# Unread products between the steps that end two attention stages, and two VectorE steps in another order

## The chip, the core and the metric

The kernel runs on one core of a Trainium2 chip. The core has a matrix engine (TensorE, "PE" in the profile, with its weight loads as "PEld"), a vector engine (VectorE, DVE), a scalar engine (ScalarE, ACT), a general engine (GpSimd, POOL) and a queue engine (SyncE, SP) that here only issues DMAs. The engines run side by side, each through its own list of instructions in order, and wait for each other by semaphores. The metric is device microseconds (us) of one execution of the whole program, the median of three.

## What is computed

Two transformer layers over 8 sequences of 1024 tokens with 128 features, in float32:

```python
x = x + attn0(layernorm(x))    # 8 heads of 32, softmax over all 1024 keys, K and V through a rank-64 latent
x = x + ffn0(layernorm(x))     # 14 experts, the best two per token, gelu, weighted sum, clip
x = x + attn1(layernorm(x))    # 16 heads of 8, linear attention, causal: cumulative sums of k v^T
x = x + ffn1(layernorm(x))     # 8 experts, the best one per token with a capacity, relu
```

The router of each expert layer takes the logits of a token, picks one or two experts, and gives every token a place in the expert's rows.

## The kernel before

**Four stages in a row.** The first attention (lines 203 to 839) works through blocks of 512 queries; its steps are laid out half-step by half-step by a hand-written table. Beside it runs the end of each sequence: output projection, norm, router. The first expert layer (`tiles0`, line 903) then works through 72 tiles of 256 rows. The second attention (lines 1049 to 1588) works through 32 pairs of 128-token chunks, and the second expert layer (`tiles1`, line 1599) through 36 tiles of 256 rows.

**How tokens get to the experts.** A token's normalised row is written to DRAM at a row number that depends on its expert and on its rank among that expert's tokens: `rows_in` in the first layer, `rows1` in the second. These moves are indirect DMAs on GpSimd, one for each chunk of 128 tokens (and each of the two choices in the first layer), in `move` (lines 602 and 1426). Their row numbers are made by `places` (588 and 1408) on VectorE: `at` in the first layer, `where1` in the second. Each expert's rows are then cut into tiles of 256, and `expert_tables` (117) makes from the counts of all tokens a table of each tile's first row and expert (`row_j`, `exp_j`). SyncE reads `row_j` to fetch a tile (`fetch`, `fetch1`), VectorE reads `exp_j` to copy the expert's weights beside it (`stage`, `stage1`). The first fetch and the first staging of each expert layer wait for the last of the moves.

**The two ends.** The end of the first attention (806 to 839) finishes the last 512 tokens. A loop over four chunks divides by the softmax's sums on VectorE (818, 819), projects on TensorE (`f.project`, 451), and gathers the norm's statistics (`norm.stats`, 271). Then come the norm's power (on GpSimd), the scaled rows (`scaled`), their transposes (`turned`, 304), and the router's pieces in the order of `choice` (617): logits, the first and second choice, counts, ranks, places, softmax weights. The eight moves left over by `places` are issued last (838). The first step of `tiles0` makes the tables.

The end of the second attention (1549 to 1588) runs the last pairs, then routes the last sequence in two halves of four chunks, `first` and `second`, each a `Route` (1336) with the pieces `logits`, `choose`, `count`, `rank`, `places`, `softmax`, `keep_top`. `scatter(4)` issues four moves. `tiles1` begins with its tables.

**What sets the order.** In the attentions and in the tile loops the order of TensorE and VectorE is the program's order (`manual_schedule`). At the first tables (line 911) it is left to the scheduler, at the second (1607) it is the program's.

Names in the profile: `op` is the projection's result, `tp` and `px` are transposes, `lg` logits, `rk` ranks, `tot` the counts summed over partitions, `both_t` the transposed table, `ph` and `py` the first and second product of an expert, `xr` a fetched tile, `wt` its expert's weights.

## Time and profile before

| | us |
|---|---|
| median of three executions | 2041.25 (2039.91 to 2042.38) |
| the profiled execution | 2055.6 |
| its span, first to last instruction | 2053.8 |
| TensorE busy, share of the span | 1941.6, 95% |
| VectorE, ScalarE, GpSimd busy | 1376.3, 1107.8, 1201.0 |
| granted TensorE clock, mean over the span | 0.955 of full speed |
| `ph` of an expert of the second layer (L1645), 288 products | 69.9, 386 ns each |

How to read it: the profile divides the span into 40 equal slices of 51.3 us. For each engine a digit gives the busy share of a slice in tenths (9 is 90% or more), and the row PEclk gives the clock that TensorE was granted, in tenths of full speed. TensorE's products are pipelined, so their durations overlap and a "busy" TensorE is not one at its peak. A row of the timeline gives the start, the duration (from the first to the last of the merged instructions), the engine, the line, the operation, what it writes and reads, partitions by elements, how many instructions were merged, and in brackets how long the engine was idle before and what released it.

### The profile page before, as it was taken

What the parts mean: (1) busy time and instruction counts of PE and PEld (TensorE: products, weight loads), DVE (VectorE), ACT (ScalarE), POOL (GpSimd) and SP (SyncE); (2) the same over time, 40 slices, a digit from 0 to 9 for tenths busy, and PEclk for the clock granted to TensorE, in tenths of its full rate; (3) what the DMA queues carried; (4) which work ended last, traced back from release to release, by engine and by line L of the source; (5) the groups of instructions that cost most, each with busy time, mean ns of one, the idle gap of its engine ahead of it and who ended that gap; (6) DMA issues with size and microseconds to landing.
All of it is one profiled execution on the core that took longest, in us unless ns stands there. A gap on an engine that the chain in (4) does not pass through costs nothing. (4 is left out here: it accounts for less than half of the span.)

```text
span 2053.8 us, 45114 instructions
## 1 busy us (share of the span) xinstructions
PE 1941.6 (95%) x17340; PEld 1002.5 (49%) x17340; DVE 1376.3 (67%) x3551; ACT 1107.8 (54%) x2338; POOL 1201.0 (58%) x1312
## 2 busy tenths in 40 slices
PE   7999999999999999999999998699499999996997
PEld 3333333333333333333333333599367666665897
DVE  6677768768767767767766776476457666654453
ACT  3555555555565555555565554366357666551443
POOL 1465656767766767767667775422455556624455
PEclk9999999999999999999999998799789999986999
DMA  7000000000000000000000000344222211101331
GB/s 240 1 2 2 1 2 4 8 8 10 8 8 9 8 8 9 8 8 9 8 8 12 8 9 27 97 132 136 62 75 81 78 43 48 51 23 52 106 107 58
DMA packets 49406, 80.92 MB, mean 39 GB/s; under 512 B 13225, under 2 KB 32112, under 8 KB 49056
## 3 DMA queue, kind: packets, MB, share of 16 engines
q0 software_dynamic: 17552, 41.03, 6.0%
q1 hardware_dynamic: 28240, 28.97, 4.9%
q10 hardware_dynamic: 3392, 7.95, 1.3%
q8 instruction: 140, 2.29, 0.5%
q14 instruction: 82, 0.67, 0.1%
HBM read 42.08 MB, written 35.96 MB: 38 GB/s over the span
## 5 line engine op out<-in xcount | busy, mean ns | idle before, releaser
L352 DVE TENSOR_REDUCE nmp<-big 128x1 f32<-128x512 f32 x1000 | 641.7, 682 | 280.6 <-PE st L388 236.7
L391 ACT ACTIVATE e<-st 128x512 f32<-128x512 f32 x1000 | 544.2, 595 | 479.9 <-PE st L388 425.0
L216 POOL TENSOR_TENSOR e<-e 128x512 f32<-128x512 f32 x488 | 604.0, 1268 | 52.8 <-PE num L405 52.7
L348 PE MATMUL big<-kT,qT 32*128 32x512 f32 x2000 | 625.9, 641 | 0.7 <-DVE nmp L352 0.4
L388 PE MATMUL st<-qT,kT 32*128 32x512 f32 x2000 | 533.5, 590 | 0.0
L405 PE MATMUL num<-e,v 128*32 128x512 f32 x3064 | 301.6, 465 | 3.1 <-ACT nums L434 1.8
L216 POOL TENSOR_TENSOR outT<-nums,dens 128x64 f32<-128x64 f32 x248 | 80.5, 325 | 343.3 <-DVE dens L423 258.1
L388 PEld LDWEIGHTS st<-qT,kT 32*128 32x128 f32 x2000 | 214.8, 192 | 5.1 <-issue 3.0
L387 PE MATMUL st<-nb,ones_h 3*128 3x512 bf16 x1000 | 212.7, 385 | 0.4 <-ACT e L391 0.4
L405 PEld LDWEIGHTS num<-e,v 128*32 128x32 f32 x3064 | 61.6, 108 | 292.4 <-issue 272.3
L348 PEld LDWEIGHTS big<-kT,qT 32*128 32x128 f32 x2000 | 192.0, 183 | 21.3 <-DVE nmp L352 17.3
L387 PEld LDWEIGHTS <-ones_h 3*128 3x128 bf16 x1024 | 50.9, 91 | 308.4 <-issue 302.6
L1122 POOL DMA_INDIRECT got<-rows_out,found x128 | 126.3, 987 | 93.7 <-PE tp L1157 36.5
L603 POOL DMA_INDIRECT rows_in<-xn,at x128 | 129.8, 1014 | 33.6 <-issue 24.9
L423 DVE RECIPROCAL dens<-dens 128x64 f32<-128x64 f32 x248 | 130.1, 536 | 16.5 <-ACT dens L418 16.4
L405 PE MATMUL den<-e,ones 128*32 128x512 f32 x1032 | 140.7, 608 | 0.0
L1667 POOL DMA_INDIRECT out_x<-y,to x72 | 78.9, 1096 | 68.2 <-DVE y L1665 51.2
L1648 ACT ACTIVATE g<-ph,wt 128x256 f32<-128x256 f32 x144 | 63.6, 474 | 86.9 <-PE ph L1645 83.2
L1083 POOL TENSOR_TENSOR rs<-ve,mhalf 128x2 f32<-128x2 f32 x64 | 46.3, 724 | 90.8 <-DVE ve L1081 65.9
L970 POOL DMA_DIRECT2D rows_out<-y x68 | 39.5, 581 | 94.5 <-DVE y L967 87.3
L1177 ACT ACTIVATE qm<-qk,cst 128x256 f32<-128x256 f32 x128 | 54.6, 496 | 53.9 <-DVE qk L1174 33.2
L1427 POOL DMA_INDIRECT rows<-row,where x64 | 63.8, 997 | 30.7 <-issue 14.3
(289 smaller groups left out, 2976.4 us busy)
## 6 DMA issues: line engine op xcount, KB each, us to landing
xr<-rows SPq DMA_DIRECT2D x36, 257.0 KB
xr<-rows_in SPq DMA_DIRECT2D x72, 128.0 KB
rows_out<-y POOLq DMA_DIRECT2D x68, 128.0 KB
nb<-part SPq DMA_DIRECT2D x384, 1.0 KB
blob<-in_blob ACTq DMA_DIRECT2D x8, 578.0 KB
blob<-in_blob SPq DMA_DIRECT2D x1, 4494.0 KB
x<-in_x SPq DMA_DIRECT2D x8, 512.0 KB
rows<-nil ACTq DMA_DIRECT2D x9, 257.0 KB
```

Source lines behind the costliest of these rows:

```text
L216: return tc.keep_in_program_order(f(*args, **kw))
L348: nc.tensor.matmul(ps, lhsT=qTs[n][r, qc * P:(qc + 1) * P], rhs=kTs[n][r, kb * BLK:(kb + 1) * BLK], start=True, stop=True,)
L352: nc.vector.tensor_reduce(nmps[n][:, h, qc, kb:kb + 1], ps, AX.X, ALU.max, negate=True)
L387: nc.tensor.matmul(st, lhsT=ones_h[r3, :], rhs=nbs[n][r3, cols], start=True, stop=False)
L388: nc.tensor.matmul(st, lhsT=kTs[n][r, kc * P:(kc + 1) * P], rhs=qTs[n][r, cols], start=False, stop=True)
L391: nc.scalar.activation(e[:, h, :], st, AF.Exp, scale=SCALE0)
L405: nc.tensor.matmul(vds[key][32 * h:32 * h + 32, cols], lhsT=ones[:, :HD0] if den else vs[b][:, kc, c0:c0 + HD0], rhs=e[:, h, cols], start= ...
L423: nc.vector.reciprocal(s[:, cols], s[:, cols])
L603: ins = nc.gpsimd.indirect_dma_start(out=rows_in, out_offset=bass.IndirectOffsetOnAxis(ap=ats[k][:, j:j + 1], axis=0), in_=xn[:, c0 + j, : ...
L1122: ins = tc.keep_in_program_order(nc.gpsimd.indirect_dma_start(out=gots[p][:, i, k, :], out_offset=None, in_=rows_out, in_offset=bass.Indir ...
L1427: ins = nc.gpsimd.indirect_dma_start(out=rows1, out_offset=bass.IndirectOffsetOnAxis(ap=at[:, c:c + 1], axis=0), in_=row[:, c, :], in_offs ...
L1667: ins = nc.gpsimd.indirect_dma_start(out=out_rows, out_offset=bass.IndirectOffsetOnAxis(ap=at[:, i:i + 1], axis=0), in_=y[:, i, :], in_off ...
```

## The change

A helper `keep_busy(bank, n)` issues `n` products on TensorE into one PSUM bank: bf16, 128 rows by 128 columns of weights, 512 moving columns, both operands read from the tile of ones. Nothing reads the bank. The helper is called

- in the loop that ends the first attention, with 2, 5, 5 and 14 products after the four projections, and with 13 after the logits (39 in all);
- in `expert_tables`, with 14 products after the sum of the counts and with 52 (first layer) or 42 (second) after the table's transposes;
- at the end of the second attention, with 5 products after the first half's logits and 11 after the second half's.

That makes 105 products at the first end and 72 at the second. The first tables are put under the program's order for TensorE and VectorE. At the second end, `second.logits()` is called after `first.places()` and `scatter(4)` instead of before them.

```diff
+    ones_b = ones.bitcast(BF16)
+
+    def keep_busy(bank, n):
+
+        for _ in range(n):
+            nc.tensor.matmul(
+                bank.rearrange("p (a b) -> p a b", a=2), lhsT=ones_b[:, :P],
+                rhs=ones_b.unsqueeze(1).to_broadcast([P, 2, 2 * P]), start=True, stop=True,
+            )
+
...
-    def expert_tables(tab, psum, ptag, counts, ne, nt):
+    def expert_tables(tab, psum, ptag, counts, ne, nt, unread, fill):
...
         nc.tensor.matmul(tot, lhsT=ones, rhs=counts, start=True, stop=True)
+        keep_busy(unread, 14)
...
         for i in range(2):
             nc.tensor.transpose(ps[:, i, :], both[:, i:i + 1], ident)
+        keep_busy(unread, fill)
...
         num, den = (vds.pop((n, qb, d)) for d in (False, True))
+        unread = sc.tile([P, BLK], F32, name="st", tag="st")
         for i in range(CPK + 1):
...
             if i:
                 f.project(i - 1, 1)
+                keep_busy(unread, (2, 2, 5, 5, 14)[i])
                 norm.stats(i - 1, 1)
...
         for piece in f.choice():
             piece()
+            if piece == f.logits:
+                keep_busy(unread, 13)
...
         if first == 0:
-            held0.tables = expert_tables(tab0, px, "px", counts, E0, NT0)
+            with tc.manual_schedule(engines={mybir.EngineType.PE, mybir.EngineType.DVE}):
+                unread = ph_ps.tile([P, BLK], F32, name="unread", tag="ph")
+                held0.tables = expert_tables(tab0, px, "px", counts, E0, NT0, unread, 52)
...
         first.logits()
+        unread = pa.tile([P, BLK], F32, name="a")
+        keep_busy(unread, 5)
         first.choose()
         first.exponentials()
...
         first.rank()
-        second.logits()
         first.places()
         scatter(4)
+        second.logits()
+        keep_busy(unread, 11)
         first.softmax()
...
                 with tc.manual_schedule(engines={mybir.EngineType.PE, mybir.EngineType.DVE}):
-                    tables.__dict__.update(expert_tables(tab, px, "px", counts1, E1, NT1).__dict__)
+                    unread = ph_ps.tile([P, BLK], F32, name="unread", tag="ph")
+                    tables.__dict__.update(expert_tables(tab, px, "px", counts1, E1, NT1, unread, 42).__dict__)
```

## The prediction

> **What bounds the kernel now.** I read three views: the page's 40 slices, one-microsecond windows of the clock, and the timeline of two stretches. The slices say where to look:

> ```profile
> PE   7999999999999999999999998699499999996997
> PEclk9999999999999999999999998799789999986999
> ```

> TensorE is busy everywhere except at the end of the first attention (25th and 26th slice), at the start of the second (29th: gathers, which the change leaves alone) and at the end of the second (37th). In the same places the granted clock falls. By one-microsecond windows it is 0.50 from 1276.97 to 1311.0, and, at the second end, from 1881.1 to 1908.4. Outside such stretches the page's tile loops run with TensorE full, so what is gained ahead of a loop moves the whole rest of the program.

> The timeline of the first end (start, duration, engine, line):

> ```profile
> 1279.02 0.80 PE L457 MATMUL op<-wo_sb,outT 128*128 128x128 f32 x2 [0.69 <-DVE outT L819]
> 1283.95 1.89 PE L480 MATMUL lg<-gate_sb,xT 128*128 128x14 f32 x8
> 1291.69 0.16 DVE L599 TENSOR_SCALAR at<-to 128x4 uint32<-128x4 f32 x1
> ...
> 1292.62 0.96 POOL L603 DMA_INDIRECT rows_in<-xn,at  x1 [4.30 <-issue]
> ...
> 1301.46 0.96 POOL L603 DMA_INDIRECT rows_in<-xn,at  x1 [0.30 <-issue]
> 1303.70 2.21 DVE L930 COPY wt<-blob 128x642 f32 x4 [8.57 <-DMA rows_in<-xn,at]
> 1305.98 1.43 PE L939 MATMUL px<-cst,xr 128*128 128x128 f32 x4 [11.26 <-DMA xr<-rows_in]
> 1307.20 2.06 PE L948 MATMUL ph<-xt,wt 128*128 128x256 f32 x4
> ```

> The reader should see a serial path: projection, norm, transposes, logits, choice, ranks, places (`at`), then eight moves on GpSimd, 1.26 us apart, their landing, the first fetch, the first tile. GpSimd ends last, not the table: `row_j` is written by 1295.0, nine microseconds before it is used. So only what makes `at` come earlier, or the tiles after 1305.98 shorter, counts.

> The second end:

> ```profile
> 1884.09 0.19 DVE L1406 TENSOR_TENSOR cand<-rk,oh 128x32 f32<-128x32 f32 x1 [1.24 <-PE rk L1404]
> 1885.76 0.19 DVE L1354 TENSOR_REDUCE mx<-lg 128x4 f32<-128x32 f32 x1 [1.48 <-PE lg L1350]
> 1886.57 0.17 DVE L1414 TENSOR_SCALAR where<-to 128x4 uint32<-128x4 f32 x1
> 1887.52 1.03 POOL L1427 DMA_INDIRECT rows<-row,where  x1 [5.90 <-ACT ex L1362]
> ...
> 1896.45 1.41 POOL L1427 DMA_INDIRECT rows<-row,where  x1 [0.30 <-issue]
> 1902.89 0.66 PE L1636 MATMUL px<-cst,xr 128*128 128x128 f32 x2 [8.89 <-DMA xr<-rows]
> 1904.84 3.62 PE L1645 MATMUL ph<-xt,wt 128*128 128x256 f32 x8
> 1908.55 1.89 PE L1645 MATMUL ph<-xt,wt 128*128 128x256 f32 x8
> ```

> Again eight moves in a row end last. Their first waits for `where`, and `where` waits only because `mx` of the second half's logits stands ahead of it on VectorE and itself waits 1.48 us for TensorE. The last two rows show one tile's products at half clock (3.62) and nearly full (1.89).

> **The change, part by part.** Everything is summed against the profiled execution (2055.6 us, span 2053.8).

> *Price of an unread product.* No row has a 128x128 bf16 product of 512 columns. The nearest:

> ```profile
> 1530.48 0.60 PE L1227 MATMUL a<-later,low 64*128 64x512 bf16 x2
> ```

> One of these lasts 387 ns (median), two 0.60 us, so they start 0.213 us apart at full clock; a pair at half clock (1491.46) takes 1.03 with 0.63 each, 0.40 apart. The weights (94 ns) load under the product before. Lower bound 0.213, upper 0.40; from that pair to the next line's product there are 0.265 a piece, which I keep as a middle. I take 0.213, if the clock is held.

> *Do they fit?* TensorE issues in order, so what follows a batch waits for it. First end: after each projection 2, 5 and 5 (0.4 to 1.1 us) stand before a projection that waits for `outT`, 1.90 us after the one before: hidden, 0.5 us left. Then 14 (3.0 us) from 1279.5 to 1282.5, where the transposes are due at 1282.5 (1282.80 less the 0.3 gained below): just hidden. 13 (2.8 us) after the logits, before `rk`, whose inputs take 3.0 us on VectorE: hidden, 0.3 left. 14 before `both_t` (due 3.7 us after `tot`): hidden. 52 (11.1 us) after `both_t` from about 1292.8: to 1303.9, first transposes due 1304.25. Second end: 5 (1.1 us) to 1881.3, transposes due 1881.4; 11 (2.3 us) to 1887.0, `rk` due 1886.7 but its second half due 1887.0: nothing; 14 hidden; 42 (8.9 us) from 1891.9 to 1900.9, transposes of tile 0 due 1900.6, but the tile products queue behind tile 1's transposes, which need a fetch at 1902.1: nothing. Every batch is within 0.5 us of its cover; without cover each 0.1 us per product costs 10.5 us at the first end's 105, 7.2 at the second's 72.

> *What the clock gives, first end.* Last projection pair 0.80 to 0.49 (the row at 1273.29 has that): 0.31. Transposes of a pair 0.66 to 0.38, logits 1.89 to 1.06 (eight passes at 1879.10, full clock): 1.11. From the end of the count's scan (1289.32) through `rk` to `cand` at 1290.13 there are 0.8, about 0.3 less at full clock. `at`, and with it all eight moves, come 1.7 us earlier. GpSimd is free for them: its five earlier moves end at 1288.3. Then the first tiles: two transpose pairs 0.3 each, `ph` of tile 0 2.06 to 1.03 (the row at 1312.24), `ph` of tile 1 1.82 to 1.03 in part: 2.1. Sum **3.8**.

> *The table's new place, first end.* The name says places go ahead of tables. In the compiled order of VectorE they do not: `grid` (0.61) and `tiles` (0.62) still stand between `ranks` and `at`, as before; only `lead`'s memset and a few table steps move behind `shares`. Had they moved, `at` would be some 0.9 us earlier. I count nothing; the table comes at most 0.3 later, with nine microseconds of cover (GpSimd's moves).

> *Second end, the order.* `second.logits` moves behind `first.places` and the four scatters. Its eight TensorE passes have the same place among TensorE's instructions, as neither step issues any there; the four scatters are the same GpSimd DMAs in the same order, and nothing passes SP's queue. On VectorE `mx` and `pr` move behind three operations of 0.2. `where` then ends 0.8 after `cand` instead of 2.65: 1.85. The clock gives `cand` another 0.45 (two transpose pairs 0.86 to about 0.44, `rk`). Sum 2.3 at the first move. `mx` loses nothing: its products end after `where`; were they done earlier it would lose 0.6. The moves stay back to back: `where` of the second half is at 1888.4, its move is not due before 1890.3.

> *Second end, tiles.* Tile 1's rows arrive 2.3 earlier, `ph` of tile 0 takes 1.73 instead of 3.62: 1.7 to 1.9. Sum **4.1**.

> Together 7.9: 2055.6 to 2047.7. The median shown is 14.4 lower (0.7%); scaled, 7.8, so 2041.25 becomes **2033.5**.

> [...]

> ```profile
> 1850.49:1853.91 3.42, 3.42 (x28) 2.88 (x26) 2.53 (x11) 0.47 (x2) 1.17 (x2) 0.98 0.00 0
> 1853.91:1857.32 3.41, 3.41 (x48) 1.61 (x50) 0.28 (x2) 0.88 (x3) 2.52 (x3) 0.50 0.22 77
> ```

> TensorE is busy for the whole first window, much of it logits of 8 columns, and the clock is halved in the next. So columns streamed count, not gaps. The unread products stream 512 each, and at the first end every 3.4 us hold at least 1.6 us of them. At the second, from 1881.3 to 1884.6 only transposes, `rk` and logits run; a window that falls on it loses the clock. Drops and rises here lie near multiples of 3.41 us from 1276.97, so I give this about 4 in 10; then the 11 take up to 1.7 more, and the 42 behind them end that much later, past their cover: 1.6 lost, 2035.1. [...] I keep 7.9 and put the rest into the range.

> **Rivals.** *Overrun (0.13).* If the pitch is 0.265, the 52 and 42 end 2.3 and 0.9 us after their covers and the others cost 1.0: gain 3.7, **2037.6**. For: covers are thin. Against: the pair's own pitch.

> *Cold filling (0.11, the slower side).* Place: the batches themselves. If the clock is already half when a batch starts, it runs at 0.40, and TensorE's order makes the chain wait. Each cold window puts a batch 1.7 us late; two windows at each end cost 6.8 and undo 3.3 of the clock's gain of 6: **2042**, and if they stay cold throughout, 0.19 on each of 177 less the covers is some 28 against 1.9 kept: 2067. It decides from a mean pitch of 0.29, that is a mean clock of 0.73 in the batches. For: in the rows 1853.9 to 1870.9 are cold right before the second end. Against: the clock is 1.00 when the first batch starts (1274), and dense products brought it back within 5 us at 1306 to 1311. With two cold windows it is about even, so I price this case at **2047**, three windows at each end.

> *Only the order counts (0.10).* Unread products neither hold nor delay: 1.9, **2039.4**. For: transposes and eight-column logits didn't hold it. Against: 512-column tiles do, throughout the first attention.

> **How the numbers follow.** Forecast as argued, 0.66, own range 2030 to 2037: the second attention has single cold windows (at 1604, 1652, 1700, 1748) whose number shifts with where it starts; one more or less is up to 1.7 us, and two either way is 3.4. Overrun and order-only reach 2039.4; one more cold window there 2041. Range 2029.5 to 2041, leaving out 0.11 for cold filling and a little below. About 0.2% (4 us) is what can be told from no change. Faster by more: 0.66 plus half of the overrun, 0.73; within: the rest of it and order-only, 0.16; slower 0.11.

> **What would show it.** Right: granted clock 1.00 from 1274 to the first tile; logits of eight passes near 1.06; first of the last eight moves near 1290.9; first tile `ph` 1.03; at the second end `where` before `mx`, first move 2.3 us sooner after its `rk`, `ph` of tile 0 near 1.75. Wrong: unread products 0.40 apart; first tile's transposes released by TensorE itself instead of by the fetch; a longer second attention with more cold windows than before.

## The result, and the profile after

The changed kernel takes **2034.91 us** (median of eight, 2027.27 to 2043.59), against 2040.58 (2037.13 to 2046.25) for eight executions of the kernel before that ran beside it. The two medians lie 5.7 us apart (0.9972); the estimated ratio on record is 0.9952, with a 95% interval of 0.9930 to 0.9973, which would be 9.8 us (5.5 to 14.3). So the change is faster, by 5 us or more, and this pair doesn't give the size any closer. The prediction said 2033.5, 7.8 less than before. The profiled execution of the changed kernel took 2033.86 us (span 2032.1, mean granted clock 0.976); that of before had a span of 2053.8 at 0.955.

The slices of the changed kernel, for TensorE and its clock:

```profile
PE   7999999999999999999999999999599999998997
PEclk9999999999999999999999999999789999988999
```

At the end of the first attention (25th and 26th slice) TensorE is now busy and the clock full. At the end of the second (37th) it is nearly so. The 29th slice, the gathers at the start of the second attention, is as before.

The timeline of the first end (start, duration, engine, line):

```profile
1276.76 3.18 PE L116 MATMUL st<-ones 128*128 128x512 bf16 x14
1280.85 1.06 PE L492 MATMUL lg<-gate_sb,xT 128*128 128x14 f32 x8
1286.41 0.62 DVE L136 TENSOR_TENSOR grid<-tot,cst 128x448 f32<-128x448 f32 x1
1287.07 0.62 DVE L141 TENSOR_REDUCE tiles<-grid 128x14 f32<-128x448 f32 x1
1287.61 0.16 DVE L611 TENSOR_SCALAR at<-to 128x4 uint32<-128x4 f32 x1
1288.53 0.96 POOL L615 DMA_INDIRECT rows_in<-xn,at  x1 [3.07 <-issue]
...
1290.92 11.38 PE L116 MATMUL unread<-ones 128*128 128x512 bf16 x52
...
1297.38 0.96 POOL L615 DMA_INDIRECT rows_in<-xn,at  x1 [0.30 <-issue]
1302.14 0.38 PE L957 MATMUL px<-cst,xr 128*128 128x128 f32 x2
1302.90 0.41 PE L957 MATMUL px<-cst,xr 128*128 128x128 f32 x2 [0.38 <-DMA xr<-rows_in]
1303.15 1.03 PE L966 MATMUL ph<-xt,wt 128*128 128x256 f32 x4
```

Four things to see. The logits take 1.06 instead of 1.89, the first tile's `ph` 1.03 instead of 2.06: full clock on the whole path (granted 1.00 from 1270 to 1310). Fourteen unread products of 0.379 us each take 3.18, so they start (3.18 - 0.379) / 13 = 0.2155 us apart. `grid` and `tiles` still stand ahead of `at`, as the prediction read from the compiled order. And the 52 end at 1302.3, where the second pair of tile 0's transposes still waits for its DMA until 1302.90: the long batch is covered, by little.

The timeline of the second end:

```profile
1865.04 0.19 DVE L1424 TENSOR_TENSOR cand<-rk,oh 128x32 f32<-128x32 f32 x1 [0.77 <-PE rk L1422]
1865.68 0.17 DVE L1432 TENSOR_SCALAR where<-to 128x4 uint32<-128x4 f32 x1
1865.73 4.22 PE L116 MATMUL a<-ones 128*128 128x512 bf16 x11
1865.91 0.19 DVE L1372 TENSOR_REDUCE mx<-lg 128x4 f32<-128x32 f32 x1
1866.63 1.03 POOL L1445 DMA_INDIRECT rows<-row,where  x1 [3.60 <-issue]
...
1875.74 0.96 POOL L1445 DMA_INDIRECT rows<-row,where  x1 [0.30 <-issue]
1883.76 0.60 PE L1658 MATMUL px<-cst,xr 128*128 128x128 f32 x4
1884.66 1.99 PE L1667 MATMUL ph<-xt,wt 128*128 128x256 f32 x8 [0.30 <-DVE xt L1660]
1886.71 1.89 PE L1667 MATMUL ph<-xt,wt 128*128 128x256 f32 x8
```

`where` now stands before `mx`, 0.64 us after `cand`. But the 11 unread products took 4.22 us where 2.5 was due. Windows of the clock show why. A window here is a step of 3.41 us, as the changes of the clock lie whole such steps apart: in the trace of before the stretches of one clock from 1276.97 on last 34.13, 143.36, 27.31, 6.83 and 20.48 us, which is 10, 42, 8, 2 and 6 steps, at 0.50, 1.00, 0.50, 1.00 and 0.50 in turn. The rows, like the pair of windows in the prediction, give start:end, length, TensorE busy, weight loads, three other engines, the granted clock, and last what the DMAs moved:

```profile
1862.68:1866.09 3.41, 2.78 (x18) 2.04 (x19) 2.30 (x14) 2.12 (x7) 0.35 (x1) 1.00 0.00 0
1866.09:1869.50 3.41, 3.41 (x10) 1.22 (x8) 1.98 (x13) 0.23 (x1) 2.26 (x3) 0.50 0.11 39
```

In the first of the two only transposes, `rk` and logits run, and at its very end the first two of the eleven; the next 3.41 us have half the clock, and the other nine fall into them. This is the loss to which the prediction gave 4 in 10.

### The profile page after: what moved, and what is told of

It reads as the page before. It is cut to its first block, busy times and chain, and to the rows that moved or that the text cites. A ratio compares the mean times of both kernels' runs of the same rounds, so it can differ in the third digit from the quotient of the medians.

```text
span 2032.1 us, 45469 instructions
## 1 busy us (share of the span) xinstructions
PE 1959.4 (96%) x17517; PEld 1007.4 (50%) x17517; DVE 1377.1 (68%) x3551; ACT 1107.7 (55%) x2338; POOL 1201.5 (59%) x1312
## 5 line engine op out<-in xcount | busy, mean ns | idle before, releaser
L399 PEld LDWEIGHTS <-ones_h 3*128 3x128 bf16 x1024 | 51.1, 91 | 308.9 <-issue 302.2
L1140 POOL DMA_INDIRECT got<-rows_out,found x128 | 126.4, 987 | 89.5 <-PE tp L1175 42.1
```

Source lines behind the costliest of these rows:

```text
L399: nc.tensor.matmul(st, lhsT=ones_h[r3, :], rhs=nbs[n][r3, cols], start=True, stop=False)
L1140: ins = tc.keep_in_program_order(nc.gpsimd.indirect_dma_start(out=gots[p][:, i, k, :], out_offset=None, in_=rows_out, in_offset=bass.Indir ...
```

## Where the 21.7 us between the two profiled executions lie

Each stage is measured between the same two instructions in both traces.

| stage (us) | before | after | difference |
|---|---|---|---|
| start to the first end's first reciprocal | 1272.6 | 1270.0 | -2.6 |
| first end: reciprocal to the first `py` | 38.5 | 35.1 | **-3.4** |
| first tiles, to the second attention's first gather | 144.9 | 144.5 | -0.4 |
| second attention, to the last sequence's first logits | 423.1 | 410.9 | -12.2 |
| second end: those logits to the second tile's `ph` | 29.4 | 26.2 | **-3.3** |
| second tiles, to the end | 145.2 | 145.4 | +0.2 |

The ends give 6.7 us. The 12.2 of the second attention lie where the change issues nothing. The experiments therefore had two questions: is the gain at the ends what the prediction says it is, and does the change do anything to the second attention?

## The experiments

They ran on three chips, a group on each, against the kernel before on the same chip (medians 2008.1, 2005.53 and 2055.55 us). The ratio is the measure, since two executions of one kernel differ by 10 us and more (before took 2001.44 to 2011.94 on the first chip). The lengths of the ends come from each run's profiled execution, and they repeat far better: the first end of a kernel that leaves it as it was took 38.5 to 38.6 us in four profiles, the second end 29.2 to 29.6 in three.

| run | ratio (95%) | us against before | clock got back, us | first end | second end |
|---|---|---|---|---|---|
| e0_before, nothing changed | | |  | 38.6 | 29.2 |
| a0_after, the change | 0.9961 (0.9947 to 0.9976) | -8.0 | 31.1 | 35.2 | 25.4 |
| e8_first, only the first end | 0.9979 (0.9966 to 0.9993) | -4.3 | 17.7 | 35.2 | 29.6 |
| e9_second, only the second end | 0.9983 (0.9965 to 1.0002) | -3.5 | 13.4 | 38.6 | 27.9 |
| e1_order, only the order | 0.9983 (0.9974 to 0.9991) | -3.4 | 0.2 | 38.6 | 27.9 |
| e2_fill, only the products | 0.9961 (0.9947 to 0.9975) | -7.8 | 28.3 | 35.1 | 26.5 |
| e3_narrow, products of 8 columns | 0.9970 (0.9957 to 0.9983) | -6.0 | 4.3 | 38.6 | 27.8 |
| e4_notable, none in the tables | 0.9980 (0.9967 to 0.9994) | -4.0 | 14.1 | 36.8 | 27.2 |
| e5_bridge, three more at the second end | 0.9939 (0.9922 to 0.9957) | -12.2 | 30.4 | 35.1 | 25.2 |
| e6_places, both `at` ahead of the table | 0.9961 (0.9950 to 0.9972) | -7.8 | 28.2 | 35.9 | 25.3 |
| e7_both, the last two together | 0.9966 (0.9955 to 0.9976) | -6.8 | 26.2 | 34.3 | 24.9 |
| e10_best, the same with a longer batch | 0.9959 (0.9943 to 0.9975) | -8.4 | 33.1 | 34.3 | 27.2 |

(The third column is the ratio less one, times the median of before in that group; the medians taken directly differ from it by up to 2 us. The fourth is from all executions: each one's span times one less its granted clock is the clock that it lost, and the column says how much less the median is than that of before, which is 88.3 us in the group of a0_after, e8_first, e9_second and e10_best, 72.3 in that of e1_order, e2_fill, e3_narrow and e5_bridge, and 70.1 in the other. It is good to about 2 us, as the clock is on record to three digits.)

The fourth column separates the kernels far better than the times do. In the profiles of before the clock is half for 34.1 us at the first end and 27.3 us at the second, which is 17.1 and 13.7 us of lost clock, 30.7 in all. The kernels with the wide products at both ends got back 26 to 33 us, e8_first 17.7, e9_second 13.4, and the order alone 0.2. Only part of it is time, as TensorE waited through much of the half clock (11.26 us ahead of the first tile's transposes at the first end, 8.89 at the second, in the prediction's lines).

### The change and its two halves: a0_after, e8_first, e9_second

a0_after is the change itself. e8_first leaves the second end as it was:

```diff
-        keep_busy(unread, 14)
+        if ne == E0:
+            keep_busy(unread, 14)
...
-        keep_busy(unread, 5)
...
+        second.logits()
         first.places()
         scatter(4)
-        second.logits()
-        keep_busy(unread, 11)
...
-                    tables.__dict__.update(expert_tables(tab, px, "px", counts1, E1, NT1, unread, 42).__dict__)
+                    tables.__dict__.update(expert_tables(tab, px, "px", counts1, E1, NT1, None, 0).__dict__)
```

e9_second does the reverse: no products in the first end's loop, after its logits or in its tables, whose order is again the scheduler's.

> The changed kernel itself on this chip, beside its parts. If the ends are all of it: first end near 35.1 against 38.6 before, second end 25.1 when no window of the clock is lost there and 26.2 when the one ahead of the ranks is, so 7.0 to 8.0 us below the median of before. If the unread products also change the second attention's windows for the better, 10 us or more below; if for the worse, less than 5.

> Only the first end's unread products and its hand-written order; the second end as before. Ends alone: first end 35.1, second end 29.2, so 3.5 us below before. If a first end that is earlier shifts the second attention's windows: anything from 0 to 8 below. Cold filling: none of it saved.

> Only the second end's part: the order and its unread products; the first end as before. Ends alone: first end 38.6, second end 25.1 to 26.2, so 3.3 to 4.3 below before, and together with the first end's run the sum of the two is the whole change within 1.5 us. If the two parts help or hinder each other, the sum is off by 3 or more.

Measured: 8.0 us for the whole, 4.3 and 3.5 for the halves, 7.8 in sum. The halves add up, though e9_second's interval reaches from -7.2 to +0.4 us, so that the times alone test this weakly; the clock got back adds up as well (17.7 and 13.4 against 31.1). The whole has the size of its two ends in its own profile (38.6 - 35.2 and 29.4 - 25.4: 7.4). In a0_after no window is lost at the second end, and that end is 4.0 us shorter: what the prediction summed for a held clock was 4.1.

e9_second shows the other case in its clearest form. Its windows (columns as above):

```profile
1867.90:1871.31 3.41, 2.03 (x24) 1.52 (x23) 1.77 (x8) 0.65 (x2) 0.90 (x2) 1.00 0.13 43
1871.31:1874.72 3.41, 3.41 (x13) 2.11 (x13) 2.95 (x18) 1.88 (x5) 0.92 (x2) 0.50 0.00 0
1874.72:1878.13 3.41, 3.41 (x18) 3.13 (x17) 0.92 (x6) 0.75 (x2) 0.39 (x1) 0.50 0.00 0
1878.13:1881.54 3.41, 3.41 (x10) 1.21 (x9) 1.95 (x12) 0.23 (x1) 2.57 (x3) 0.50 0.22 77
1881.54:1884.95 3.41, 3.41 (x21) 1.95 (x20) 2.19 (x11) 0.00 (x0) 1.84 (x2) 1.00 0.25 81
```

The clock is halved for exactly three windows of 3.41 us. TensorE counts as busy in all three. The first two hold the batch of five and the start of the eleven among transposes, ranks and logits and do not bring the clock back; the third, filled by most of the eleven, does. What the slow eleven delay can be read from the timeline of the same run: the second half's ranks, its places, and with them the fifth move:

```profile
1877.63 4.45 PE L116 MATMUL a<-ones 128*128 128x512 bf16 x11
1881.61 0.96 POOL L1440 DMA_INDIRECT rows<-row,where  x1 [0.30 <-issue]
1883.13 0.17 DVE L1427 TENSOR_SCALAR where<-to 128x4 uint32<-128x4 f32 x1
1884.07 0.96 POOL L1440 DMA_INDIRECT rows<-row,where  x1 [1.49 <-issue]
1886.82 9.23 PE L116 MATMUL unread<-ones 128*128 128x512 bf16 x42
1895.89 0.60 PE L1653 MATMUL px<-cst,xr 128*128 128x128 f32 x4
```

GpSimd waits 1.49 us for `where` (0.30 between moves is its usual step), and tile 0's transposes start right behind the 42. That end took 27.9 us, 2.5 more than a0_after's and as much as with the order alone (e1_order, 27.9): in this execution the products of the second end bought nothing. It is the prediction's rival of cold filling, at one end and in one execution: still faster than before, by what the order gives, and not slower.

### The order and the products apart: e1_order, e2_fill

e1_order is the kernel before with this alone:

```diff
-        second.logits()
         first.places()
         scatter(4)
+        second.logits()
```

e2_fill is the change without it: `second.logits()` and the eleven stand again ahead of the places.

> The kernel before, with only the second half's logits moved behind the first half's places and scatters on VectorE; no unread products. Stage lengths of the profile are compared: the first end from the first reciprocal of the divide loop to the first py of the expert tiles (38.5 us before, 35.1 changed), the second end from the last sequence's first logits to the second tile's ph (29.5 before, 26.2 changed). Clock theory: first end stays 38.5, second end 27.6 (1.9 less), clock 0.50 at both ends; whole program about 2 us less, not to be told from no change. Rival, only the order counts: the whole difference between the two kernels, 6 to 10 us, is already here.

> The changed kernel with the second half's logits back ahead of the first half's places; the unread products stay. Clock theory: first end 35.1, second end 27.1 if the clock is held and 28.1 if it is lost for a window, 5 to 6 us less than before as a whole. Rival, only the order counts: both ends as before, no gain.

From the last sequence's first logits to the start of `where` there are 7.47 us before, 5.64 with the order alone, 6.21 with the products alone and 5.17 with both. So the order is worth 1.83 at half clock, as the prediction had it (1.85), but only 1.04 once the clock is full (6.21 to 5.17); the products are worth 1.26 without the order and 0.47 with it. The sum is safe, the shares depend on which is taken first. The order cannot carry the gain: in e1_order's profile the end is 1.3 us shorter and the clock is lost as before, and over all executions the order alone gets back 0.2 us of clock where the products alone get back 28.3. The ratio of the run with the products alone is as good as that of the whole change.

### Does any product hold the clock? e3_narrow

Each unread product is replaced by two with 8 moving columns:

```diff
-        for _ in range(n):
-            nc.tensor.matmul(
-                bank.rearrange("p (a b) -> p a b", a=2), lhsT=ones_b[:, :P],
-                rhs=ones_b.unsqueeze(1).to_broadcast([P, 2, 2 * P]), start=True, stop=True,
-            )
+        for _ in range(2 * n):
+            nc.tensor.matmul(bank[:, :8], lhsT=ones_b[:, :P], rhs=ones_b[:, :8], start=True, stop=True)
```

> The changed kernel with each unread product of 512 columns replaced by two of 8 columns, so that TensorE still issues products without a long gap but streams hardly any columns. Theory that streamed columns hold the clock: the clock falls to 0.50 at both ends as before, first end 37 to 40 us, second end 27.6 or more. [...]

The timeline of its first end, TensorE alone:

```profile
1268.23 0.41 PE L116 MATMUL st<-ones 128*128 128x8 bf16 x10
1270.40 0.93 PE L116 MATMUL st<-ones 128*128 128x8 bf16 x28
1273.59 1.12 PE L316 MATMUL tp<-cst,xn 128*128 128x128 f32 x4 [2.26 <-ACT xn L308]
```

The clock falls at 1268.3, 4.9 us after the first reciprocal; in the profiles without products it fell 4.3 to 5.1 us after it. All steps of the first end have the lengths of before (38.6 in all), and the second end those of the order alone. So 354 extra TensorE instructions hold nothing, and it isn't for a long pause: in the 4.9 us before the fall TensorE never paused for more than 0.86 us. All nine executions agree: their mean granted clock is 0.962 to 0.969, as in e1_order (0.961 to 0.969), against 0.977 to 0.979 in e2_fill. The run does not separate columns from busy time: the 28 take 0.93 us where 14 wide ones take 3.18, and TensorE idles 2.26 us behind them. For that the row of e9_second stands, where TensorE was busy through two windows and the clock did not return. The time is a weaker witness: 6.0 us less than before can't be told from e2_fill's 7.8, though the ends of e3_narrow's profile explain only 1.6 of it; where the rest comes from is open.

### The products in the tables: e4_notable

```diff
-        keep_busy(unread, 14)
...
-        keep_busy(unread, fill)
```

> The changed kernel without the unread products in the tables (14 and 52, 14 and 42), with all others kept. Theory: places and moves stay 1.5 us (first end) earlier than before, but the clock is lost in the wait for the moves and the first tiles run at half clock: first end 37.1 (35.1 plus 2.0), second end 27.9 (26.2 plus 1.7). Rival, the clock of the tiles has another cause or the products of the tables only delay the first tile: first end 35 or less.

The choice and the ranks keep their full-clock lengths at both ends. The clock then goes after `both_t`, and the first tiles lose it: `px` to the first `py` is 4.88 us at the first end instead of 2.95, the two tiles' `ph` at the second are 3.48 apart instead of 1.95. The ends are 1.6 and 1.7 us longer than a0_after's, 3.3 in all; by the ratios the difference is 4.0. So the 122 products in the tables buy almost half of the whole, and what they buy is the first tiles, as the prediction's sums of 2.1 and 1.7 to 1.9 had it. The clock got back says the same: 14.1 us of some 31.

### Bridging the second end, and the places really ahead of the table: e5_bridge, e6_places, e7_both, e10_best

e5_bridge fills the stretch that the prediction called weak:

```diff
         first.logits()
-        keep_busy(unread, 5)
+        keep_busy(unread, 6)
...
         back_transposed(p - 1)
+        keep_busy(unread, 2)
         first.count()
         back_transposed(p)
```

e6_places orders `grid` behind the last `at` and has 45 products instead of 52:

```diff
-        nc.vector.tensor_tensor(
+        ins = nc.vector.tensor_tensor(
...
+        if ne == E0:
+            behind(ins.ins, last_at[0])
...
+                    last_at[:] = [ins.ins.name]
...
-                held0.tables = expert_tables(tab0, px, "px", counts, E0, NT0, unread, 52)
+                held0.tables = expert_tables(tab0, px, "px", counts, E0, NT0, unread, 45)
```

e7_both has both edits, and e10_best has at the first end 20 products behind `tot` instead of 14 as well.

> The changed kernel with the unread products after the first half's logits at 6 instead of 5, and 2 more between the two transposed pairs of the second end, so that no 3.4 us hold less than about 1.4 us of 512-column products. Theory: the clock is no longer lost at the second end, the 11 products take 2.5 us instead of 4.2, the second end is 25.7 (0.5 less than the changed kernel's 26.2). Rival, the loss has nothing to do with the missing columns: the clock falls again in that place, 26.2 or, as the two more delay the ranks, 26.6.

> The changed kernel with the tables' first step ordered behind the places on VectorE at the first end, as the change's name says, and 45 instead of 52 unread products behind the table, as the moves end earlier and the table later. Theory: the row numbers come 0.9 us earlier, and with them eight moves and the first tile: first end 34.2 against 35.1. Rival, something else ends last there (the table's later transposes): 35.1 or more.

> The places ahead of the tables with 45 products, and the bridged second end (6, and 2 more between the transposes), together. Theory: first end 34.2, second end 25.7, about 1.4 us less than the changed kernel, which the timing can't tell from it; against the kernel before 0.993 to 0.997. Rival, the gains hide each other or move the clock's loss elsewhere: not better than the changed kernel by the stage lengths.

> The kernel with the bridge of two and with both places ahead of the table at the first end, and 20 instead of 14 products behind the totals, so that the pause of 1.96 us ahead of the transposed row shrinks to some 0.7. If that pause let the clock go in the places run (the 45 took 11.56 instead of 9.87), it holds here: the 45 in 9.9, first end 34.3, and the median 8 to 10 below before, about 1 below the changed kernel's. Rival: the pause had nothing to do with it; then the 45 are slow again in a profile that falls so, and the median is that of the run with both, 7 to 8 below before.

The bridge: the second end took 25.2 and 24.9 us, against 25.4 in a0_after, which held the clock without it. In e10_best the clock was already half when that end began and stayed so until 1889.2; the bridge's 6 and 2 then took 2.72 and 1.06 us instead of 1.45 and 0.59 (e5_bridge), and the end took 27.2. Four profiles held the clock through the weak stretch without the bridge (a0_after, e2_fill, e4_notable, e6_places), so one profile each of e5_bridge and e7_both cannot say what it is worth: e5_bridge's 12.2 us is the best ratio of all, but e7_both has the same bridge and 6.8.

The places: both `at` come 0.66 us earlier (from `cand` to the first `at` 0.90 instead of 1.57), and e7_both's and e10_best's first ends are 34.3 instead of 35.1, as was expected of e6_places (34.2). The prediction put this at 0.9. In e6_places itself the same edit lost more than it gave, so that its first end took 35.9:

```profile
1280.10 3.18 PE L116 MATMUL unread<-ones 128*128 128x512 bf16 x14
1285.24 0.53 PE L168 MATMUL both_t<-cst,both 128*1 128x128 f32 x2 [1.96 <-DVE both L162]
1285.61 11.56 PE L116 MATMUL unread<-ones 128*128 128x512 bf16 x45
1297.01 0.60 PE L961 MATMUL px<-cst,xr 128*128 128x128 f32 x4
```

The table is later now, so TensorE idles 1.96 us ahead of `both_t`. One window of 3.41 us fell onto that pause (1.46 us busy in it); in the next the clock was half, the 45 took 11.56 instead of 9.87, and the first transposes start right behind them, 1.5 us later than in e5_bridge as counted from SyncE's issue. In e7_both, with the same pause, no window was lost:

```profile
1289.14 0.53 PE L168 MATMUL both_t<-cst,both 128*1 128x128 f32 x2 [1.96 <-DVE both L162]
1289.51 9.87 PE L116 MATMUL unread<-ones 128*128 128x512 bf16 x45
```

What differs between the two profiles is where the windows fall. Counted in steps of 3.41 us from a change of the clock in the same trace, e6_places has one from 1282.88 to 1286.30, and the pause (1283.28 to 1285.24) lies wholly in it; in e7_both a window ends at 1288.18, in the middle of the pause (1287.18 to 1289.14), and the two windows hold 2.42 and 2.45 us of work. e10_best, with the pause shortened by six products, kept it too, which after e7_both proves nothing. In time none of the four can be told from the change: the intervals overlap widely, and 0.8 us is below what these comparisons resolve. No version was found that is surely better.

### The second attention

The second attention is taken from the first gather to the last sequence's first logits. The clock that it lost is its length times one less its granted clock:

| run (group) | length, us | clock lost, us |
|---|---|---|
| before, after (the pair above) | 423.1, 410.9 | 50.4, 42.7 |
| e1_order, e2_fill, e3_narrow, e5_bridge (first) | 373.1, 382.5, 379.4, 380.5 | 26.9, 35.7, 33.8, 35.5 |
| e0_before, e4_notable, e6_places, e7_both (second) | 372.0, 378.5, 381.4, 381.8 | 23.2, 31.9, 35.1, 35.3 |
| e9_second, e8_first, a0_after, e10_best (third) | 418.2, 420.5, 425.0, 433.1 | 42.1, 51.1, 50.4, 62.9 |

Within a group a longer second attention is one that lost more clock (e8_first and a0_after, 0.7 us apart in lost clock, are the exception). The kernels without products have the shortest in the first two groups, by 6 us and more, the reverse of the pair above; in the third all four have products, and they span 15 us. e0_before's and e1_order's profiled executions were also among the shortest of their kernels (1996.45 and 1995.43 us, where the medians are 2005.5 and 2004.2).

All executions together say more than these profiles. If the change lost or saved clock in the second attention, the clock got back would not be that of the two ends. It is 31.1 us for a0_after against the 30.7 of the ends, 17.7 for e8_first against 17.1, and 13.4 for e9_second against 13.7. In the other two groups e2_fill, e5_bridge, e6_places and e7_both have 28.3, 30.4, 28.2 and 26.2, a little less than the ends and not more. And a0_after's 8.0 us leave 0.6 for all that lies outside the ends. So the 12.2 us of the pair is not borne out as an effect of the change; most of it is a different draw of a scatter that the stage has in every group. Between the groups the stage differs by some 40 us, of which the lost clock is under 20; what the rest is was not looked for.

## Why the prediction was right

**Price and cover.** 0.213 us was taken from a pair of another shape; 0.2155 was measured, so the overrun at 0.265 is out. At half clock the weight loads of e9_second's eleven stand 0.43 us apart; the upper bound of 0.40 was low. The covers held, in so far as the clock did.

**First end, 3.8 predicted, 3.4 measured.** Term by term: projection 0.31, measured 0.26 (reciprocal to the norm's power 8.37 to 8.11); transposes and logits 1.11, measured 1.08; ranks 0.3, measured 0.29 (end of the scan to `cand`, 0.81 to 0.52); places 0, measured 0; first tiles 2.1, measured 2.03. What is missing is small and was not in the sum: the choice, from `mx` to the scan, took 0.1 longer (3.02 to 3.14, and 3.12 or 3.13 in every kernel with wide products there; why was not looked for), and 0.1 was given back between the last move and the fetch.

**Second end, 4.1 predicted.** Where the clock held, 4.0 in a0_after and 4.1 to 4.5 in the three others with the products and the order (e5_bridge to e7_both, two of them with the bridge, against 29.4 before). In the changed kernel's own profile it did not hold, and 3.3 remained. `where` was 2.3 earlier as summed; the tiles gave the rest less what the late 42 took.

**The weak stretch.** Six profiles have the second end's wide products and no bridge. Five of them came to it at full clock, and one of these (after) lost a window there: fewer than 4 in 10, though five are few. In e9_second the clock fell within the first 0.5 us of the end, and in e10_best, with the bridge, it was half already, a case that the prediction had under cold filling. The price was put at 1.6; it was 0.8, and where the end began cold 2.5 (e9_second) and 1.8 (e10_best, which has the bridge), measured against a0_after. This is the one size that the forecast's central number left out and the range held.

**The rivals.** Only the order counts: out, by e2_fill and e8_first, and by e1_order's clock. Overrun by pitch: out. Cold filling: seen as a mechanism in e6_places and e9_second, at 1.5 to 2.5 us for a place, with three cold windows at one end (e9_second) and never at both, as the prediction priced it. Its sum there is off: two windows at each end are 7.9 less 6.8 less 3.3, 2.2 us slower, so 2043.4 and not 2042, and three by the same sum 2048.5 and not 2047.

**What went ahead of the falls.** In e6_places the clock fell behind a window with a pause of 1.96 us, in e7_both it held across a pause as long; in e3_narrow it fell behind no pause over 0.86, and in e9_second the window before the fall had 1.4 us without work in all and the two cold ones none. So the length of a pause does not tell the falls apart here. The prediction's reading, that the columns streamed count, fits these rows and its own pair of windows; how many it takes they do not say. Counted in steps of 3.41 us over both ends, and one window ahead of each, of all fourteen profiles, the fifteen falls to half clock came behind windows in which no wide product started (thirteen), two (after) or five (e6_places), and none behind six or more. But just ahead of the second end e9_second lost the clock behind a window with 2.03 us of work and no wide product (its row above), and a0_after kept it behind one with 2.06. Where the steps lie against the work differs from profile to profile: the pause of 1.96 us lay wholly in one of them in e6_places (1282.88 to 1286.30), and across two in e7_both, with a boundary at 1288.18.

**Luck.** The median came out 1.4 us from the forecast. Eight executions that spread over 16 us do not fix it that well, so the nearness is in part luck; what stands behind it are the lengths of the ends and the clock got back, and the 8.0 us of a0_after's 22 executions.

**What stays open.** The four runs of the first group are 1.4 to 4.5 us better than their ends explain, those of the others from 2.0 worse to 2.1 better. Whether the first group's common median of before came out high was not tried.

## What to carry to other kernels

Where TensorE's clock is lost on a serial path, work that nobody reads can hold it (the wide products at both ends got back 26 to 33 us of clock), and is free as long as each batch fits into a wait that ends later by something else (the 52 of the changed kernel ended 0.6 us ahead of such a wait's end); size it by the measured start-to-start time (0.2155 us here), and count what the batch costs at half clock (0.43 apart), because what stands behind it in TensorE's order then waits (the ranks of e9_second for an eleven of 4.45 us, those of a0_after for one of 2.53). Look for the stretches that no batch covers: a window lost on one made the eleven behind it take 4.22 us in the changed kernel's profile. Split a measured gain by stages between fixed instructions before believing it; here more than half of the difference between two profiled executions came from a stage that the change does not touch. Where every execution's granted clock is on record, compare that too: it told the kernels apart where their times did not.
